# Four graph layers in one kernel: layer 2's second pass split in two, and the tangent sums centred by a matrix product

## The chip, the cores and the metric

The kernel runs on one core of a Trainium2 chip. The metric is device time in microseconds. Eight runs of the kernel before gave a median of 1151.43 us, from 1147.78 to 1156.36; one further execution was profiled.

## The reference

A matrix `x` of 4096 rows and 64 columns goes through four layers over one adjacency matrix `adj` of 4096 x 4096 zeros and ones (float32). Each layer's result is added to its input and every row is normalised.

```python
x = _layernorm(x + _L0_gnn_ref(x, adj, L0_gnn_W, L0_gnn_b), axis=-1)
x = _layernorm(x + _L1_gnn_ref(x, adj, L1_gnn_r, L1_gnn_w_att, L1_gnn_b_att), axis=-1)
x = _layernorm(x + _L2_gnn_ref(x, adj, L2_gnn_weight, L2_gnn_bias), axis=-1)
x = _layernorm(x + _L3_gnn_ref(x, adj, L3_gnn_att_w, L3_gnn_att_b), axis=-1)
```

Layer 0 averages the neighbours and multiplies by a weight. Layers 1 and 3 are hyperbolic attention: for every pair of rows a sigmoid of two scores, times the edge, weights a logarithm map of one row at the other; the weighted sum is a tangent, along which the row is then moved. Layer 2 weights a row's last neighbours by powers of one half, by their rank from the end of the row:

```python
support = input @ weight
mask = (adj != 0).astype(support.dtype)
rank = jnp.cumsum(mask, axis=1)
deg = rank[:, -1:]
k = jnp.minimum(deg, float(MAX_NEIGH))
pos = rank - (deg - k)
w = mask * jnp.where(pos > 0, DECAY ** (k - pos), 0.0)
out = w @ support + bias
```

## The kernel before, in words

The output rows are cut into four groups of 1024 (`GROUPS`, taken 3, 2, 1, 0) and the neighbours into 32 blocks of 128 (`BLOCKS`, taken 31 down to 0). `adj` lies transposed in memory, neighbours on partitions. `load` (L653) brings two blocks of one group, 1 MB, by SP's queue into one of six buffers; a layer needs 64 loads. Float32 edges are read as their upper bfloat16 halves. On 64 of the 256 loads, in layers 0 and 2, `check` (L739) has DVE test that all edges are 0 or 1 (L741).

**Layers 1 and 3.** `attend` (L914) works on one group: per block PE makes a score `z` [128, 1024] of three products for each half (L935, L938, L941), ACT a sigmoid (L943) and a square (L946), and DVE joins them (L949, and L951 for two blocks at once); PE then adds the weighted rows into `acc` [128, 512] (L955), the group's two halves above each other on the partitions. At the group's end ACT copies `acc` to `sums` (L962). `move` (L972) turns `sums` to rows by four PE transposes (L969), has ACT copy them out of PSUM (L985), forms `u` by taking each row's mean away (L988 reduce, L989 scale, L991 subtract, DVE), multiplies x by u (L992, POOL), squares u (L994, ACT), and after two reduces (L997, L999) runs a long chain of small operations on [128, 8] tiles, with `rsqrt` (L673 to L679) three times, to the new rows (L1067 POOL, L1068 and L1071 DVE). The sum of a row before centring is also used (L1001). Layer 1's rows then go through `linear` (L1074) into layer 2's `halves`; layer 3's go out by DMA (L1377).

**Layer 2.** Two groups are taken together, 3 and 2 in the first pass, 1 and 0 in the second. For each group and block PE counts in `z` [128, 1024], which is never cleared within a pass: the block before is passed by and this block enters, two products of 512 columns each (L1340). ACT makes the weights 2^-count by one exponential of 1024 (L1349), and PE adds `halves` times weights into the group's `acc` by four products, one group later (L1356, through `lag`). So each count waits for the exponential that read the same `z` before, and the two groups are two independent chains. `end_2` (L1288) turns the sums to rows (L969), adds bias and input, `norm_rows` (L761) normalises, and `prepare` (L781) makes the rows ready for layer 3: casts (L798 to L800), turned copies `hi_lo`, `lo_hi`, `src`, `dst` (L842 on PE, L846 on ACT), two logarithms (L849, L850), the scores, and for group 3 `left_b` (L904, L910).

**Order.** Row work is written as generators. `later` puts one into one of two queues, `tick` advances them a step each at fixed places of the block loops, `yield n` waits n ticks, and `need(tag)` runs them until a group's rows are ready. `take` and `free` share two PSUM buffers of one bank, `aux`, among them. In layers 0 and 2 PE and ACT follow the order as written (`tc.manual_schedule`); otherwise a planner orders each engine's instructions by its own estimates. Each engine then runs its list in order. The tiles of row work have one buffer each, so that a move's `u` is free only when the move before has used it up.

Of the kernel before, what the change touches and what calls it, by code (L numbers as in the profile page):

```python
# [10 lines left out]
F32 = mybir.dt.float32  # L11
# [47 lines left out]
def gnn_stack_kernel(  # L59
# [509 lines left out]
    def stream(fits):  # L569

        with ExitStack() as st:
# [127 lines left out]


# [271 lines left out]
            def move(layer, s, sums, curve):  # L972
# [7 lines left out]
                sum_1, k, d, uu = nums("sum_1"), nums("k"), nums("d"), nums("uu")  # L980
                u, w, sq, of = grp("u"), grp("w_att"), grp("sq"), grp("z0")
                yield from free()
                t = to_rows_of(sums)
                yield near()
                nc.scalar.copy(of.rearrange("p (h k) f -> p h k f", h=2), t)  # L985
                held.pop()
                yield near()
                V.tensor_reduce(sum_1, of, AX.X, ALU.add)  # L988
                V.tensor_scalar(k, sum_1, 1.0 / D, None, ALU.mult)  # L989
                yield soon()  # L990
                V.tensor_sub(u, of, over(k))  # L991
                nc.gpsimd.tensor_mul(w, xg, u)  # L992
                yield after(12)
# [315 lines left out]
            lag = []  # L1309

            def flush():

                while lag:
                    lag.pop(0)()

            with tc.manual_schedule(engines=FIXED):
                for n in range(0, NW, 2):
                    two = GROUPS[n : n + 2]
                    zs = [ps.tile([P, WW], F32, name="z") for _ in two]

                    accs = [[] for _ in two]
                    behind = [None, None]
                    for g in reversed(range(NB // 2)):
                        edges = []
                        for s in two:
                            a, edge = load(s, g)
                            if g % 2 == 1:
                                junk = sb.tile([P, 2, WW], F32, name="t").bitcast(BF16)
                                check(s, g, a, junk[:, 0, :].rearrange("p (b i) -> p b i", b=2))
                            edges.append(edge)  # L1330
                        need((2, 2 * g // WB))
                        for k in (1, 0):
                            j = 2 * g + k
                            for i, edge in enumerate(edges):
                                z, acc = zs[i], accs[i]
                                here = edge[:, k * WW : (k + 1) * WW]
                                for lhs, rhs in ((pass_by, behind[i]), (enter, here)):
                                    for h in range(0, WW, W):
                                        if rhs is not None:
                                            nc.tensor.matmul(  # L1340
                                                z[:, h : h + W], lhs, rhs[:, h : h + W],
                                                start=j == BLOCKS[0], stop=True,
                                                skip_group_check=True,
                                            )
                                behind[i] = here
                                flush()

                                w = sb.tile([P, 2, WW], F32, name="sq").bitcast(BF16)[:, 0, :WW]
                                nc.scalar.activation(w, z, AF.Exp, bias=at_edge, scale=-LN2)  # L1349

                                def add(acc=acc, j=j, w=w):
                                    if not acc:
                                        acc.append(ps.tile([P, W], F32, name="acc"))
# [112 lines left out]
```

## Time and profile before

| | us |
|---|---|
| median of eight runs | 1151.43 |
| lowest and highest of them | 1147.78, 1156.36 |
| the profiled execution | 1147.65 |
| its span | 1145.9 |
| layer 2, first pass and second pass (ends of the ACT copies L1370) | 104, 119 |
| layer 3, its four groups (ends of the ACT copies L962) | 105, 84.4, 80.9, 81.1 |
| after the last of them | 33.5 |

The span is what the profile covers; the execution's own time is 1.75 us longer. Engines are named as in the profile: PE is TensorE's matmul, PEld its weight load, DVE VectorE, ACT ScalarE, POOL GpSimd, SP the queue that issues the loads. A number in square brackets behind a row of the timeline is the idle time of the engine before that instruction, with the instruction that ended it.

### The profile page before, as it was taken

The numbers are of one execution on the slowest core, as the hardware profiler recorded it, in microseconds if no ns is written. First come the engines' busy times: TensorE is split into PE (matmuls) and PEld (weight loads), VectorE is DVE, ScalarE is ACT, GpSimd is POOL, SyncE is SP. The second block draws the span as 40 slices with busy tenths as digits, with TensorE's granted clock in tenths as the row PEclk, the third lists the DMA queues.
The fourth block names the chain that finished last, engine by engine and source line by source line (L and its number), as shares of the span: only waits on it lengthen the run. The fifth ranks groups of instructions, "written<-read, shape, count | busy, mean of one in ns | idle before, by whom it ended". The sixth has DMA issues, their size and how long they took to land.

```text
span 1145.9 us, 13431 instructions
## 1 busy us (share of the span) xinstructions
PE 1007.2 (88%) x4832; PEld 387.4 (34%) x4917; DVE 961.2 (84%) x1901; ACT 812.2 (71%) x823; POOL 61.1 (5%) x97
## 2 busy tenths in 40 slices
PE   6899897899899999988999988998798999999870
PEld 3445544233333333332333232333333333333220
DVE  6587898999999899989773584349988999999996
ACT  0003215899989788977767688887987999889860
POOL 0020120000000000000000020001000000000001
PEclk9999998999999999999999999999898999999995
DMA  9999998556566466644988886785355666666400
GB/s 351 421 379 411 364 414 321 202 169 217 198 208 219 162 209 208 216 172 149 322 298 301 324 305 242 258 339 184 110 183 174 222 209 209 219 209 207 150 0 22
DMA packets 38418, 271.57 MB, mean 237 GB/s; under 512 B 4550, under 2 KB 4550, under 8 KB 5574
## 3 DMA queue, kind: packets, MB, share of 16 engines
q1 hardware_dynamic: 37440, 269.50, 65.2%
q10 hardware_dynamic: 902, 1.12, 0.3%
q8 instruction: 40, 0.66, 0.2%
q14 instruction: 36, 0.29, 0.1%
HBM read 269.55 MB, written 1.05 MB: 236 GB/s over the span
## 4 chain that ended last, share of the span: by engine, by line
DVE 57%; PE 26%; ACT 6%; DMA 5%; issue 3%; POOL 2%; ACTq 0%; POOLq 0%; SPq 0%; DVEq 0%
DVE t L951 21%; DVE t L949 21%; PE z L1340 9%; PE acc L1356 5%; DMA edges<-in_adj_dram 4%; PE acc L955 3%; PE acc L1229 2%; DVE junk L741 2%; ACT sq L946 2%; ACT sq L1349 1%; PE z L938 1%; PE z L935 1%; PE z L941 1%; PE aux L1092 1%; DVE rs_t L677 1%
## 5 line engine op out<-in xcount | busy, mean ns | idle before, releaser
L943 ACT ACTIVATE sig<-left_b,right 128x1024 f32<-128x1024 f32 x256 | 293.9, 1149 | 45.1 <-DVE t L949 34.4
L949 DVE SCALAR_TENSOR_TENSOR t<-z,sig 128x1024 f32<-128x1024 f32 x256 | 310.2, 1217 | 14.9 <-ACT sq L946 14.1
L946 ACT ACTIVATE sq<-z,turn 128x1024 f32<-128x1024 f32 x256 | 281.6, 1106 | 28.0 <-PE z L941 25.8
L951 DVE SCALAR_TENSOR_TENSOR t<-sq,t 128x2048 f32<-128x2048 f32 x128 | 293.0, 2289 | 0.7
L955 PE MATMUL acc<-t,xe 128*64 128x512 f32 x1024 | 257.8, 616 | 34.1 <-DVE t L951 30.4
L935 PE MATMUL z<-edges,two_i 128*128 128x512 bf16 x464 | 183.9, 396 | 20.2 <-DVE t L949 20.0
L938 PE MATMUL z<-lo_hi,hi_lo 128*128 128x512 f16 x512 | 196.1, 383 | 3.7 <-issue 0.7
L941 PE MATMUL z<-dst,src 74*128 74x512 f16 x512 | 196.6, 384 | 0.0
L1349 ACT ACTIVATE sq<-z,at_edge 128x1024 bf16<-128x1024 f32 x128 | 141.9, 1114 | 55.2 <-PE z L1340 54.1
L955 PEld LDWEIGHTS acc<-t,xe 128*64 128x64 f32 x1024 | 63.5, 137 | 170.1 <-DVE t L951 89.3
L741 DVE SCALAR_TENSOR_TENSOR t<-edges 128x2048 bf16<-128x2048 f32 x32 | 73.8, 2313 | 46.8 <-DMA edges<-in_adj_dram 46.6
L935 PEld LDWEIGHTS <-two_i 128*128 128x128 bf16 x512 | 50.5, 99 | 141.0 <-issue 97.5
L1229 PE MATMUL acc<-edges,first 128*128 128x512 bf16 x241 | 76.8, 395 | 24.3 <-DMA edges<-in_adj_dram 23.8
L1356 PE MATMUL acc<-sq,halves 128*64 128x512 bf16 x512 | 80.1, 392 | 16.6 <-ACT sq L1349 15.3
L1229 PE MATMUL acc<-edges,third 128*65 128x512 bf16 x256 | 79.8, 393 | 0.6
L741 DVE SCALAR_TENSOR_TENSOR junk<-edges 128x2048 bf16<-128x2048 f32 x32 | 73.2, 2286 | 7.1 <-DMA edges<-in_adj_dram 6.9
L1340 PE MATMUL z<-edges,enter 128*128 128x512 bf16 x247 | 76.5, 388 | 0.3
L1340 PE MATMUL z<-edges,pass_by 128*128 128x512 bf16 x235 | 74.8, 394 | 1.8 <-issue 1.7
L938 PEld LDWEIGHTS <-hi_lo 128*128 128x128 f16 x512 | 50.6, 99 | 69.7 <-issue 26.5
L941 PEld LDWEIGHTS <-src 74*128 74x128 f16 x512 | 49.7, 97 | 69.7 <-issue 5.8
L1356 PEld LDWEIGHTS <-halves 128*64 128x64 f16 x512 | 19.2, 108 | 72.4 <-issue 72.3
L1229 PEld LDWEIGHTS <-first 128*128 128x128 bf16 x256 | 24.1, 98 | 52.7 <-issue 25.3
(260 smaller groups left out, 758.7 us busy)
## 6 DMA issues: line engine op xcount, KB each, us to landing
edges<-in_adj_dram SPq DMA_DIRECT2D x256, 1024.0 KB, 5.8
x<-in_x_dram SPq DMA_DIRECT2D x4, 256.0 KB
out_dram<-x ACTq DMA_DIRECT2D x4, 256.0 KB, 4.1
w_sb<-in_L_gnn_W_dram ACTq DMA_DIRECT2D x1, 32.0 KB, 4.7
given<-in_L_gnn_b_dram ACTq DMA_DIRECT2D x1, 0.2 KB
given<-in_L_gnn_bias_dram ACTq DMA_DIRECT2D x1, 0.2 KB
given<-in_L_gnn_b_att_dram ACTq DMA_DIRECT2D x1, 0.0 KB
given<-in_L_gnn_att_b_dram ACTq DMA_DIRECT2D x1, 0.0 KB
```

Of the source, the lines that this page charges most:

```text
L741: V.scalar_tensor_tensor(junk, a, 0.0, a, ALU.not_equal, ALU.not_equal, accum_out=odd[:, n : n + 1])
L935: nc.tensor.matmul(half, two_i, edge[:, at : at + W], start=True, stop=False)
L938: nc.tensor.matmul(half, hi_lo[:, of], lo_hi[:, to], start=False, stop=False)
L941: nc.tensor.matmul(half, src[:, of], dst[:, to], start=False, stop=True)
L943: nc.scalar.activation(sig, left_b, AF.Sigmoid, bias=right[:, j : j + 1])
L946: nc.scalar.activation(sq[:, k], zp, AF.Square, bias=turn, scale=-1.0 / UNIT)
L949: V.scalar_tensor_tensor(t[:, k], zp, 0.0, sig, ALU.max, ALU.mult)
L951: V.scalar_tensor_tensor(t, sq, HIGH**2, t, ALU.add, ALU.mult)
L955: nc.tensor.matmul(acc[h * D : (h + 1) * D, :], xe[:, j, :], t[:, k, h * W : (h + 1) * W], start=j == BLOCKS[0], stop=j == BLOCKS[-1],)
L1229: nc.tensor.matmul(accs[h][:m], lhs[:, j, :], edge[:, at : at + W], start=j == BLOCKS[0], stop=j == BLOCKS[-1],)
L1340: nc.tensor.matmul(z[:, h : h + W], lhs, rhs[:, h : h + W], start=j == BLOCKS[0], stop=True, skip_group_check=True,)
L1356: nc.tensor.matmul(acc[0][h * D : (h + 1) * D, :], halves[:, j, part * D : (part + 1) * D], w[:, h * W : (h + 1) * W], start=j == BLOCKS[0 ...
```

## The change

It has two parts. In layer 2 the first pass stays as it is (`wide_pass`). The second is split into two passes, for group 1 and then for group 0 (`narrow_pass`). In a narrow pass the group's two halves of 512 are the two chains: each has a `z` of its own with two count products per block and an exponential of 512, and the four add products of a block follow one block later. There is one tick per block, as there was one per group and block. `end_2` of group 1 is queued at the end of its own pass, thus ahead of group 0's.

In `move`, the four transposes, the reduce, the scale and the subtract are replaced by four products of `sums` with a constant matrix `centre` [128, 2, 65], that holds for each half the identity less 1/64 in 64 columns and ones in the last. So PSUM holds the centred row and its sum, 260 float32 for two of the four products; these go in two parts, each with an `aux` buffer and an ACT copy of its own, into one tile of [128, 8, 65], of which `u` and `sum_1` are views.

```diff
@@ -695,6 +695,16 @@
             V.tensor_scalar(two_i, ident, 2.0 * UNIT, None, ALU.mult)
             turn = num(keep, "turn", 1)
             V.memset(turn, ROOT + OFF)
+            centre = keep.tile([P, 2, D + 1], F32, name="centre")
+            V.memset(centre, 0.0)
+            for h in range(2):
+                of = slice(h * D, (h + 1) * D)
+                V.tensor_scalar(
+                    centre[of, h, :D], ident[of, of], -1.0 / D, None, ALU.add
+                )
+                V.memset(centre[of, h, D:], 1.0)
 
 
 
@@ -977,20 +987,24 @@
                 least = 1e-15 if layer == 1 else 1e-30
                 at = blocks(s)
                 xg, x2g = x_of(layer)[:, at, :], x2[:, at]
-                sum_1, k, d, uu = nums("sum_1"), nums("k"), nums("d"), nums("uu")
-                u, w, sq, of = grp("u"), grp("w_att"), grp("sq"), grp("z0")
-                yield from free()
-                t = to_rows_of(sums)
-                yield near()
-                nc.scalar.copy(of.rearrange("p (h k) f -> p h k f", h=2), t)
-                held.pop()
-                yield near()
-                V.tensor_reduce(sum_1, of, AX.X, ALU.add)
-                V.tensor_scalar(k, sum_1, 1.0 / D, None, ALU.mult)
-                yield soon()
-                V.tensor_sub(u, of, over(k))
+                k, d, uu = nums("k"), nums("d"), nums("uu")
+                w, sq = grp("w_att"), grp("sq")
+                all_u = row.tile([P, WB, D + 1], F32, name="u_1")
+                u, sum_1 = all_u[:, :, :D], all_u[:, :, D]
+                for part in range(2):
+                    yield from free()
+                    t = take(F32, P, 2, 2, D + 1)
+                    for i in range(2):
+                        cols = slice((2 * part + i) * P, (2 * part + i + 1) * P)
+                        nc.tensor.matmul(t[:, i], sums[:, cols], centre, start=True, stop=True)
+                    yield near()
+                    nc.scalar.copy(
+                        all_u.rearrange("p (h k) f -> p k h f", h=2)[:, 2 * part : 2 * part + 2], t
+                    )
+                    held.pop()
+                    yield near()
                 nc.gpsimd.tensor_mul(w, xg, u)
-                yield after(12)
                 nc.scalar.activation(sq, u, AF.Square)
                 yield near()
                 yield soon()
@@ -1306,68 +1320,98 @@
                 yield from norm_rows(3, s, z, x2[:, blocks(s)])
                 yield from prepare(3, s, att3, batt3_sb, curve3, 1e-30, good[:, 1], 40)
 
-            with tc.manual_schedule(engines=FIXED):
-                for n in range(0, NW, 2):
-                    two = GROUPS[n : n + 2]
...
+            def wide_pass(two):
+                zs = [ps.tile([P, WW], F32, name="z") for _ in two]
+                accs = [None, None]
+                behind, lag = [None, None], []
+                for g in reversed(range(NB // 2)):
+                    edges = [load_2(s, g) for s in two]
+                    need((2, 2 * g // WB))
+                    for k in (1, 0):
+                        j = 2 * g + k
+                        for i, edge in enumerate(edges):
+                            here = edge[:, k * WW : (k + 1) * WW]
+                            count(zs[i], behind[i], here, j, WW)
+                            behind[i] = here
+                            while lag:
+                                lag.pop(0)()
+                            w = weights_of(zs[i], WW)
+                            def add(i=i, j=j, w=w):
+                                if accs[i] is None:
+                                    accs[i] = ps.tile([P, W], F32, name="acc")
+                                add_up(accs[i], j, w[:, :W], w[:, W:])
+                            lag.append(add)
+                            if two[0] != GROUPS[0] or j < BLOCKS[4]:
+                                tick(1)
+                lag.pop(0)()
+                return accs
+            def narrow_pass(s):
+                zs = [ps.tile([P, WW], F32, name="z") for _ in range(2)]
+                acc = ps.tile([P, W], F32, name="acc")
+                behind, lag = [None, None], []
+                for g in reversed(range(NB // 2)):
+                    edge = load_2(s, g)
+                    for k in (1, 0):
+                        j = 2 * g + k
+                        w = sb.tile([P, 2, WW], F32, name="sq").bitcast(BF16)[:, 0, :WW]
+                        for h in range(2):
+                            here = edge[:, k * WW + h * W : k * WW + (h + 1) * W]
+                            count(zs[h], behind[h], here, j, W)
+                            behind[h] = here
+                            weights_of(zs[h], W, w[:, h * W : (h + 1) * W])
+                        if lag:
+                            add_up(acc, *lag.pop(0))
+                        lag.append((j, w[:, :W], w[:, W:]))
+                        tick(1)
+                add_up(acc, *lag.pop(0))
+                return [acc]
+            def load_2(s, g):
+                a, edge = load(s, g)
+                if g % 2 == 1:
+                    junk = sb.tile([P, 2, WW], F32, name="t").bitcast(BF16)
+                    check(s, g, a, junk[:, 0, :].rearrange("p (b i) -> p b i", b=2))
+                return edge
+            def count(z, behind, here, j, n):
+                for lhs, rhs in ((pass_by, behind), (enter, here)):
+                    for h in range(0, n, W):
+                        if rhs is not None:
+                            nc.tensor.matmul(
+                                z[:, h : h + W], lhs, rhs[:, h : h + W],
+                                start=j == BLOCKS[0], stop=True, skip_group_check=True,
+                            )
+            def weights_of(z, n, w=None):
+                if w is None:
+                    w = sb.tile([P, 2, WW], F32, name="sq").bitcast(BF16)[:, 0, :n]
+                nc.scalar.activation(w, z[:, :n], AF.Exp, bias=at_edge, scale=-LN2)
+                return w
+            def add_up(acc, j, *ws):
+                for part in range(2):
+                    for h, w in enumerate(ws):
+                        nc.tensor.matmul(
+                            acc[h * D : (h + 1) * D, :],
+                            halves[:, j, part * D : (part + 1) * D], w,
+                            start=j == BLOCKS[0] and part == 0,
+                            stop=j == BLOCKS[-1] and part == 1,
+                        )
             with tc.manual_schedule(engines=FIXED):
+                for some in (GROUPS[:2], GROUPS[2:3], GROUPS[3:]):
+                    accs = wide_pass(some) if len(some) == 2 else narrow_pass(some[0])
+                    for s, acc in zip(some, accs):
                         sums = row.tile([P, W], F32, name="sums", bufs=2)
+                        nc.scalar.copy(sums, acc)
                         later(end_2(s, sums))
```

`load_2`, `count`, `weights_of` and `add_up` hold the statements that stood in the loop before.

## The prediction

> **What bounds the kernel now.** I read the engine totals, then the busy time by stage, cut where an accumulator is copied out (ACT L962, L1370), then the timeline inside the stages that the change touches.
>
> ```profile
> PE 1007.2 (88%) x4832; PEld 387.4 (34%) x4917; DVE 961.2 (84%) x1901; ACT 812.2 (71%) x823; POOL 61.1 (5%) x97
> ```
>
> No engine bounds the whole. The stage rows give start:end, length, then busy us of PE, PEld, DVE, ACT and POOL:
>
> ```profile
> 537.00:641.00 104.00, 100.63 (x533) 33.59 (x544) 62.77 (x180) 72.26 (x74) 4.41 (x3) 1.00 0.85 297
> 641.00:761.00 120.00, 106.71 (x602) 35.59 (x613) 58.79 (x167) 95.78 (x98) 7.35 (x16) 0.99 0.80 285
> 761.00:866.00 105.00, 89.29 (x421) 34.24 (x427) 98.83 (x188) 91.72 (x93) 7.33 (x16) 0.93 0.54 186
> 950.40:1031.30 80.90, 75.74 (x327) 26.44 (x331) 80.77 (x117) 72.38 (x72) 2.32 (x2) 1.00 0.62 211
> 1112.40:1145.90 33.50, 0.93 (x5) 0.50 (x5) 22.37 (x128) 1.96 (x4) 4.38 (x3) 0.55 0.05 19
> ```
>
> Rows one and two are layer 2's passes: PE leads, DVE works only half the time. Rows three and four are layer 3's first and third attention group: DVE leads, and the first takes 24 us more than the third, because groups 1 and 0 are still being prepared there. The last row is the tail: one group's row arithmetic with PE done.
>
> The timeline shows layer 2's rhythm (start, length, engine, line):
>
> ```profile
> 690.41 0.62 PE L1356 MATMUL acc<-sq,halves 128*64 128x512 bf16 x4
> 690.97 0.63 PE L1340 MATMUL z<-edges,pass_by 128*128 128x512 bf16 x2
> 691.97 0.62 PE L1356 MATMUL acc<-sq,halves 128*64 128x512 bf16 x4
> 692.14 1.11 ACT L1349 ACTIVATE sq<-z,at_edge 128x1024 bf16<-128x1024 f32 x1 [0.45 <-PE z L1340]
> ...
> 700.46 1.28 ACT L943 ACT_TABLE_LOAD   x1
> ...
> 705.38 0.62 PE L1356 MATMUL acc<-sq,halves 128*64 128x512 bf16 x4 [3.03 <-ACT sq L1349]
> ```
>
> One block of one group takes 1.56 us (690.41 to 691.97): 1.00 for four count matmuls, 0.56 for four adds. ACT waits 0.45 per block, so PE sets the pace until ACT runs something else: at 700.46 a sigmoid of layer 3 comes between two exponentials with a table load on each side, and PE waits 3.03. The second pass is 64 x 1.56 = 100 plus 19: four such waits (2.56, 3.03, 2.27, 2.34) make 10.2, PE's own row work and restarts the rest.
>
> The tail by timeline:
>
> ```profile
> 1121.56 0.69 DVE L1071 TENSOR_TENSOR x<-u,w_att 128x512 f32<-128x512 f32 x1 [0.93 <-POOL w_att L1067]
> 1122.29 0.69 DVE L991 TENSOR_TENSOR u<-z,k 128x512 f32<-128x512 f32 x1
> 1123.12 1.26 POOL L992 TENSOR_TENSOR w_att<-x,u 128x512 f32<-128x512 f32 x1 [1.59 <-DVE u L991]
> 1124.42 0.69 DVE L999 TENSOR_REDUCE d<-w_att 128x8 f32<-128x512 f32 x1 [1.44 <-POOL w_att L992]
> ```
>
> Group 1's move ends at 1122.25, 11.9 after the last DVE L951 (1110.31), and group 0's u can only be formed then, though its sums had been turned by 1114.3.
>
> **What the Trainium skill says.** "ScalarE: Activation LUTs", What ACT_TABLE_LOAD costs, gives 1283 ns for a load plus a drain of about 1380. The load agrees (1283 at L943, L849 and L1349); the drain does not show: the load at 700.46 is followed by its sigmoid at 701.75. The same section prices an activation with a pointer bias at 280 ns + 0.833 per element, with an overlap of 93 ns: 1133 for 1024 elements, where the trace has 1114 (L1349). For 512, which the trace lacks, it gives 706; scaled to the trace I take 0.69 us, and 0.62 less overlap. "TensorE: Matmul & The Clock Gate", Part 1, says that PE falls to half clock after an idle window of about 3.4 us. The trace agrees loosely: after the 3.03 wait the next pairs of count matmuls take 0.93 and 1.05 instead of 0.61.
>
> **The change, part by part.** The orders come from the built instruction streams.
>
> 1. Layer 2's last two groups go one after the other. The 64 loads, 32 checks (L741) and PE's count and add matmuls are as many as before; SP takes group 1's 16 loads and then group 0's, at the same 3.12 us per load and through the same six buffers, so I cost the queue at nothing; PE's pace hides it, and if the DMA fell behind the price would be its lag. What changes is ACT and the distance between a half and its next use.
> (a) 128 exponentials of 512 take the place of 64 of 1024. ACT needs 0.69 + 0.62 = 1.31 per block, not 1.11; slack falls from 0.45 to 0.25. A half's loop is 0.5 of count, 0.15 to the last matmul's end, 0.1 to ACT, 0.69 and 0.06 back (as 705.32 to 705.38): 1.5 against the 1.56 that PE needs; the second half also queues behind the first's exponential, some 0.04 over. 64 x 0.04 = 2.5; bounds 0 and 10.
> (b) ACT's row work now lands on PE. Each 1.0 us copy of turned rows (L846) left no PE gap of 0.6 before; now it costs an estimated 0.3 beside PE's own 0.46 of transposes: 12 copies, 3.6. Three sets of casts (L798 to L800, 1.55 each) add 0.5 each: 1.5. The four table stalls lengthen by 0.3: 1.2.
> (c) Group 1's rows come into layer 2: PE 4 x 0.46 + 0.2 (L854) + 0.6 (L969) = 2.6, and a Ln with one table load at the very end, 1.0. One pass boundary more: 0.8.
> Sum +13; some of (b) is absorbed where transposes and copy meet, so I take **+11**, bounds +4 and +28.
>
> 2. Layer 3's first group then prepares group 0 alone. One group's DVE work there is eleven wide operations less overlap, 6.3, and about 55 small ones at 0.1: 12, half of the 24 excess; ACT loses a Ln/sigmoid pair of loads (2.6) inside it. DVE was on the path, so **-12**, bounds -7 and -16. Late next: group 0's rows, which are needed for the last four loads.
>
> 3. Each move (L972) loses a reduce (L988, 0.68), a scale (0.15) and a subtract (L991, 0.69) on DVE: 1.3 after overlap. Three moves run in layer 1's attention groups and three in layer 3's, where DVE is busy 80.77 of 80.90: 6 x 1.3 = 7.8. Against it, DVE's new order does the moves earlier: in layer 1 and layer 3 each, some 35 small operations of group 1's move come back into the attention groups (before: after the last block), 2 x 35 x 0.075 = 5.2 if none hides. PE is busy 75.74 of the same 80.90, so not all saved DVE time is time. Net -2.6; I take **-4**, since the two POOL waits behind L992 (1.4 each, DVE idle) can also be covered; bounds -14 and +4. ACT gains 2 x 0.38 (as L1102) for 0.58, +0.18 a move; PE turns by four 128x130 float32 products for four transposes of 0.66 together: the nearest row (L1186, 271 ns against 272) says no change, bounds 0 and +0.6 each, under ACT's copy. POOL reads u with a stride: 0, up to +0.3. The centre's constants are six small DVE operations at the start, +0.3, under the first load.
>
> 4. The tail. Group 1's move has only its last quarter left after the last block: three rsqrt steps to its final u took 4.2 (1134.31 to 1138.50) and the rest to 1140.85 2.35, so u is free 6.5 after the last L951 instead of 11.9. The ACT copies into u, waiting for that, take 0.76, as L991 did. **-5.4**, bounds -2 and -7.
>
> Sum: 11 - 12 - 4 - 5.4 = -10.4. The profiled execution is 1147.65 (span 1145.9), so 1137.3; the median of the runs, 1151.43, stands 3.8 above it, and I carry the difference over: 1141. A measurement of this kernel tells about 0.3%, 3.5 us.
>
> **Rivals.**
> A. Forecast: narrow passes cost some 11, returned by layer 3 and the tail: 1141, chance 0.50, own range 1134 to 1148.
> B. The narrow loops hold PE's pace and DVE's POOL waits at a move's start go too: passes +5, moves -10, tail and layer 3 as above: -22, **1129**. For it: ACT has 0.25 of slack and DVE is the bound in six groups. Against: PE is busy for 94% of such a group. Chance 0.23.
> C. ACT becomes the bound in the narrow passes. If a half's return costs 0.3 more than PE's 1.56 (a hand-over of 0.2 for my 0.1 and 0.06, and half clock after each stall), 64 x 0.3 = 19 come on top of 11: +30 - 21.4 = +8.6, **1160**. It decides from 0.17 us per block (10.4/64) as no gain at all. For it: 1.5 of 1.56 is close and 1.0 us copies stand in the same queue. Against: PE, not ACT, waited in no clean block. Chance 0.15.
> D. The passes do not do what they say for the end: DVE's order delays group 1's or 2's rows, PE waits for them in layer 2 as it did at 798.80 (2.9) in layer 3, and layer 3's gain is paid ahead: passes +18, **1148 to 1152**. Chance 0.12.
>
> **Numbers.** B and the lower three quarters of A are faster by over 0.3% with part of D: 0.72; same 0.12 (D, A's edge, C's lower part); slower 0.16. The range 1125 to 1156 leaves out C's upper half and B's far end.
>
> **What would show it.** Per block PE at 1.56 to 1.65 in the narrow passes, and the two together 125 to 137 long (120 before); the exponential of 512 at 0.69; the first group of layer 3 near 93; later groups near 80; DVE's L1013 within 9 us of the last L961 (14.1 before); one table load fewer. I am wrong if PE waits for ACT in most narrow blocks, if it waits for rows there, or if the groups of layers 1 and 3 do not shorten.

## The result, and the profile after

The kernel after took 1143.6 us in the median of 21 runs (1137.23 to 1146.7), beside 1151.75 for 58 runs of the kernel before: a ratio of 0.9926, 95% interval 0.9913 to 0.994. The gain of 8.2 us is real and small; 1141 was predicted. Its profiled span is 1140.3 us, for 1145.9 before. The profiles differ by 5.6 and the medians by 8.2, because the profiled execution of the kernel before lay some 4 us below its median and that of the kernel after 1.5 below.

The engine totals of the kernel after:

```profile
PE 1013.5 (89%) x4864; PEld 391.5 (34%) x4949; DVE 956.8 (84%) x1882; ACT 820.8 (72%) x894; POOL 66.2 (6%) x97
```

Again no engine bounds the whole. DVE lost 4.4 us of busy time and ACT gained 8.6. The busy time by stage, kernel after, with the columns of the prediction's stage rows (start:end, length, PE, PEld, DVE, ACT, POOL, then granted clock, DMA share, GB/s):

```profile
539.90:644.70 104.80, 102.72 (x544) 34.46 (x554) 54.39 (x138) 72.96 (x77) 4.31 (x3) 1.00 0.84 302
644.70:705.60 60.90, 54.08 (x304) 18.52 (x310) 45.21 (x141) 49.47 (x80) 8.86 (x16) 1.00 0.84 295
705.60:776.60 71.00, 59.95 (x336) 20.00 (x341) 30.09 (x92) 62.34 (x94) 2.73 (x8) 0.93 0.70 242
776.60:867.70 91.10, 81.72 (x376) 29.74 (x383) 88.05 (x126) 83.55 (x83) 3.18 (x8) 1.00 0.58 199
949.00:1030.10 81.10, 76.63 (x332) 26.95 (x336) 79.96 (x114) 72.68 (x72) 4.88 (x2) 1.00 0.62 211
1115.00:1140.30 25.30, 1.53 (x9) 1.05 (x9) 15.18 (x83) 1.49 (x4) 4.15 (x3) 0.55 0.07 25
```

Layer 2's second pass of 119.1 has become two of 60.9 and 70.9, 12.7 longer together. Layer 3's first group, 105 before, takes 91.1. So the two effects of the split nearly cancel. The third group is as long as before. Cut at the last DVE operation of the last block (L961 here, L951 before), which no later step can move, the table is:

| us, one profile each | before | after | difference |
|---|---|---|---|
| layer 0 | 181.7 | 183.6 | +1.9 |
| layer 1, four groups | 356.0 | 356.3 | +0.3 |
| layer 2, first pass | 104.9 | 104.8 | -0.1 |
| layer 2, groups 1 and 0 | 119.1 | 131.8 | +12.7 |
| layer 3, group 3 | 105.0 | 91.2 | -13.8 |
| layer 3, groups 2, 1 and 0, to the last L961 | 243.7 | 243.0 | -0.7 |
| from there to the end | 35.6 | 29.6 | -6.0 |

Layer 0 has nothing new but the five small DVE operations that build `centre` (0.66 us together). It took 179.5 to 185.1 in the kernels profiled here, both ends in kernels that have `centre`, so its +1.9 can't be put down to the edit.

The rhythm of a narrow pass, from the kernel after's timeline:

```profile
656.84 0.62 PE L1401 MATMUL acc<-sq,halves 128*64 128x512 bf16 x4
...
658.11 1.27 ACT L1395 ACTIVATE sq<-z,at_edge 128x512 bf16<-128x512 f32 x2 [0.29 <-PE z L1386]
...
658.41 0.62 PE L1401 MATMUL acc<-sq,halves 128*64 128x512 bf16 x4
...
659.69 1.27 ACT L1395 ACTIVATE sq<-z,at_edge 128x512 bf16<-128x512 f32 x2 [0.31 <-PE z L1386]
```

A clean block is still 1.57 us (656.84 to 658.41), and ACT, with two exponentials in 1.27, still waits 0.3 for PE. The lost time is elsewhere, where ACT has other work. First, at group 3's casts:

```profile
663.99 1.54 DVE L805 TENSOR_TENSOR y<-x,ym 128x512 f32<-128x512 f32 x1
...
665.56 0.62 ACT L808 CAST ys<-y 128x512 f16<-128x512 f32 x1 [1.47 <-DVE y L805]
...
667.85 0.39 PE L1386 MATMUL z<-edges,pass_by 128*128 128x512 bf16 x1 [2.55 <-ACT sq L1395]
```

ACT reached the casts before DVE had made their input. It stood for 1.47 and then cast for 1.56, with the next exponentials queued behind, so PE stood for 2.55. Second, at layer 3's sigmoids, which the planner puts into this pass:

```profile
706.82 1.28 ACT L953 ACT_TABLE_LOAD   x1
708.12 1.15 ACT L953 ACTIVATE sig<-left_b,right 128x1024 f32<-128x1024 f32 x1
709.28 1.28 ACT L1395 ACT_TABLE_LOAD   x1
...
711.32 0.58 PE L1386 MATMUL z<-edges,pass_by 128*128 128x512 bf16 x1 [2.71 <-ACT sq L1395]
...
719.07 0.58 PE L1386 MATMUL z<-edges,pass_by 128*128 128x512 bf16 x1 [3.04 <-ACT sq L1395]
```

A sigmoid and two loads keep ACT from layer 2 for 3.7 us, twice. After each wait PE's matmuls start at 0.58 apiece, where 0.39 is the usual.

The tail of the kernel after; its last L961 ends at 1110.70:

```profile
1116.44 0.69 DVE L1085 TENSOR_TENSOR x<-u,w_att 128x512 f32<-128x512 f32 x1 [0.94 <-POOL w_att L1081]
1117.23 0.38 ACT L1002 COPY u<-aux 128x260 f32<-128x260 f32 x1 [2.24 <-DVE x L1085]
...
1117.50 0.38 ACT L1002 COPY u<-aux 128x260 f32<-128x260 f32 x1
...
1117.96 1.18 POOL L1007 TENSOR_TENSOR w_att<-x,u 128x512 f32<-128x512 f32 x1 [1.55 <-ACT u L1002]
...
1119.17 0.69 DVE L1013 TENSOR_REDUCE d<-w_att 128x8 f32<-128x512 f32 x1 [0.54 <-POOL w_att L1007]
```

Group 1's move gives up `u` 6.4 after the last block (1117.13; 11.9 before), the centred rows are copied in at once, and L1013 starts 8.5 after the last block, for 14.1 before.

### The profile page after: what moved, and what is told of

Read it like the earlier page. It is cut to its first block, busy times and chain, and to the rows that moved or that the text cites. A ratio compares the mean times of both kernels' runs of the same rounds, so it can differ in the third digit from the quotient of the medians.

```text
span 1140.3 us, 13541 instructions
## 1 busy us (share of the span) xinstructions
PE 1013.5 (89%) x4864; PEld 391.5 (34%) x4949; DVE 956.8 (84%) x1882; ACT 820.8 (72%) x894; POOL 66.2 (6%) x97
## 3 DMA queue, kind: packets, MB, share of 16 engines
HBM read 269.55 MB, written 1.05 MB: 237 GB/s over the span
## 4 chain that ended last, share of the span: by engine, by line
DVE 55%; PE 27%; ACT 9%; DMA 4%; POOL 2%; issue 2%; ACTq 0%; SPq 0%; POOLq 0%; DVEq 0%
DVE t L959 21%; DVE t L961 20%; PE z L1386 9%; PE acc L1401 5%; DMA edges<-in_adj_dram 4%; PE acc L1243 3%; PE acc L965 3%; ACT sig L953 2%; DVE junk L751 2%; ACT sq L956 2%; ACT sq L1395 2%; PE aux L1106 1%; PE z L945 1%; POOL sq L778 1%; PE aux L852 1%
## 5 line engine op out<-in xcount | busy, mean ns | idle before, releaser
L961 DVE SCALAR_TENSOR_TENSOR t<-sq,t 128x2048 f32<-128x2048 f32 x128 | 293.0, 2289 | 0.7
L965 PE MATMUL acc<-t,xe 128*64 128x512 f32 x1024 | 255.4, 612 | 29.6 <-DVE t L961 24.4
L948 PE MATMUL z<-lo_hi,hi_lo 128*128 128x512 f16 x512 | 193.8, 379 | 3.3 <-issue 0.3
L951 PE MATMUL z<-dst,src 74*128 74x512 f16 x512 | 195.0, 381 | 0.0
L1395 ACT ACTIVATE sq<-z,at_edge 128x512 bf16<-128x512 f32 (+1 forms) x192 | 152.8, 830 | 50.7 <-PE z L1386 48.3
L1386 PE MATMUL z<-edges,pass_by 128*128 128x512 bf16 x242 | 87.2, 398 | 16.9 <-ACT sq L1395 15.8
L1386 PE MATMUL z<-edges,enter 128*128 128x512 bf16 x239 | 83.9, 392 | 0.3
L951 PEld LDWEIGHTS <-src 74*128 74x128 f16 x512 | 49.1, 96 | 67.4 <-issue 2.1
L1081 POOL TENSOR_TENSOR w_att<-x,p 128x512 f32<-128x512 f32 x8 | 12.9, 1616 | 497.3 <-DVE q L1079 497.3
```

Source lines behind the costliest of these rows:

```text
L948: nc.tensor.matmul(half, hi_lo[:, of], lo_hi[:, to], start=False, stop=False)
L951: nc.tensor.matmul(half, src[:, of], dst[:, to], start=False, stop=True)
L961: V.scalar_tensor_tensor(t, sq, HIGH**2, t, ALU.add, ALU.mult)
L965: nc.tensor.matmul(acc[h * D : (h + 1) * D, :], xe[:, j, :], t[:, k, h * W : (h + 1) * W], start=j == BLOCKS[0], stop=j == BLOCKS[-1],)
L1386: nc.tensor.matmul(z[:, h : h + W], lhs, rhs[:, h : h + W], start=j == BLOCKS[0], stop=True, skip_group_check=True,)
L1395: nc.scalar.activation(w, z[:, :n], AF.Exp, bias=at_edge, scale=-LN2)
```

## The experiments

Ratios are to the kernel before on the same chip, with 95% intervals.

**Each part alone.** e1_centre_only is the kernel before with the new `move`; layer 2 keeps its second pass of two groups. e2_narrow_only has the two narrow passes and the old `move`. Against the kernel after:

```diff
 # e1_centre_only: layer 2 as before
-                for some in (GROUPS[:2], GROUPS[2:3], GROUPS[3:]):
-                    accs = wide_pass(some) if len(some) == 2 else narrow_pass(some[0])
+                for n in range(0, NW, 2):
+                    two = GROUPS[n : n + 2]
...
 # e2_narrow_only: move as before
-                        nc.tensor.matmul(t[:, i], sums[:, cols], centre, start=True, stop=True)
...
+                t = to_rows_of(sums)
...
+                V.tensor_reduce(sum_1, of, AX.X, ALU.add)
+                V.tensor_scalar(k, sum_1, 1.0 / D, None, ALU.mult)
...
+                V.tensor_sub(u, of, over(k))
```

> Centring product in the moves, layer 2 as before (two wide passes). Theory T (the split of the pass pays back in layer 3's first group what it costs in layer 2, and the net gain is the shorter move in the tail): layer 2's second pass 119, layer 3's first group 104, tail after the last block 30 instead of 35.6; total 0.5% below before, some 1145. Rival R1 (the gain comes from preparing group 1 in layer 2, the centring only moves work around): within 0.2% of before, 1150 or more. Rival R2 (both parts give about half): 1147 to 1148.

> Narrow passes for groups 1 and 0, moves as before (transposes, reduce, scale, subtract). Theory T: passes together 131, layer 3's first group 91, everything else as before: 1150 to 1151, a difference of 0.1% from before that cannot be told. R1: 0.7% below before, 1144. R2: 1147 to 1148.

e1 took 1142.89, 0.9923 (0.9901 to 0.9945); e2 took 1151.97, 1.0004 (0.9988 to 1.0021). In this kernel the whole gain belongs to the centring, and the split is worth nothing. Their stage rows, first e1 (second pass, then layer 3's first group):

```profile
644.90:767.60 122.70, 110.15 (x599) 35.94 (x609) 58.78 (x167) 95.19 (x97) 7.34 (x16) 0.94 0.76 277
767.60:872.10 104.50, 86.83 (x419) 32.38 (x425) 99.27 (x189) 91.62 (x95) 7.33 (x16) 0.97 0.51 187
```

and e2 (group 0's narrow pass after 62.0 for group 1's, then layer 3's first group):

```profile
708.10:779.00 70.90, 60.01 (x336) 20.08 (x341) 30.04 (x92) 62.16 (x93) 2.39 (x8) 0.93 0.66 240
779.00:870.20 91.20, 81.81 (x377) 29.76 (x383) 88.16 (x126) 83.66 (x84) 3.17 (x8) 1.00 0.55 200
```

The two stages together are 227.2 in e1 and 224.1 in e2, for 224.1 before and 223.0 after. What leaves layer 3's first group turns up in layer 2: in layer 3's first group DVE has 99.27 us of work in e1 and 88.16 in e2. From layer 3's second group to the end e1 takes 272.5, as the kernel after does (272.6), and e2 280.2 (279.3 before). This difference lies after the last block: up to there the four kernels take 242.9, 243.0, 242.6 and 243.7.

**Are DVE's two saved operations the gain?** e4_two_more_dve gives each move of the kernel after a reduce and a subtract whose results nothing reads.

```diff
                 nc.scalar.activation(sq, u, AF.Square)
+                spare, unused = nums("spare"), grp("unused")
+                V.tensor_reduce(spare, u, AX.X, ALU.add)
+                V.tensor_sub(unused, u, over(spare))
```

> The changed kernel, with a reduce and a subtract of 128x512 put back on DVE in each of the eight moves; nothing reads their results. Theory D (DVE sets the attention groups' pace, the saved operations are time): 1.3 for each of six moves and for the one in the tail, 8 to 10 above the changed kernel, 1152. Rival P (the groups are paced by the ring of PE, ACT and DVE with slack at DVE; the saved operations were covered): 0 to 3 above, 1144 to 1147.

It took 1145.78, 0.9948 (0.9932 to 0.9964): 2.2 us above the kernel after, with intervals that overlap. That lies within rival P's 0 to 3, far from theory D's 8 to 10. The profile tells more. Layer 3's groups 2, 1 and 0, up to the last block:

```profile
869.69:1114.96 245.27, 225.02 (x963) 78.76 (x977) 242.35 (x364) 211.50 (x205) 7.15 (x5) 0.99 0.50 179
```

The eight kernels profiled here that have the new move, with one buffer for `u`, take 242.8 to 243.0 for this. So three moves' two operations, 4.1 us of DVE's time, cost 2.3, and the fourth move adds 0.6 after the last block. Layer 1, with three moves too, took 354.2, not more but 2.1 less. So the operations have a price in layer 3, about half of their duration, and none that shows in layer 1. With both put back, layer 3 from its second group to the end takes 275.5, still 3.8 below the 279.3 before. So they are less than half of the centring's gain there. Whether the rest comes from the scale, the shorter way from PSUM to `u`, the `yield after(12)` that fell away or the order that the planner then finds, no run tells apart.

**Is the tail's gain the early `u`?** e8_before_two_u gives the kernel before a second buffer for `u` and `w_att`, so that group 0's `u` needn't wait for group 1's move.

```diff
-                u, w, sq, of = grp("u"), grp("w_att"), grp("sq"), grp("z0")
+                u, w, sq, of = grp("u", 2), grp("w_att", 2), grp("sq"), grp("z0")
...
-                    at, rest = blocks(s), grp("u")
+                    at, rest = blocks(s), grp("u", 2)
```

> The kernel before with two buffers each for u and w_att in the moves, nothing else. Theory U (the tail is bound by the single u: the last group's move can only begin when the move before has used it up): the tail after the last block falls from 35.6 to 28 to 30, total 5 to 8 below before, 1144. Rival O (it is DVE's planned order that puts the last group's operations behind; the buffer only follows it): tail within 2 of 35.6, total within 3 of before.

It took 1150.56, 1.0004 (0.9981 to 1.0027). The stretch after the last block did fall from 35.6 to 29.7, the kernel after's own value. But layer 3's third group rose from 80.9:

```profile
952.30:1038.20 85.90, 79.08 (x333) 27.08 (x331) 83.34 (x125) 72.81 (x72) 4.91 (x2) 0.96 0.56 199
```

DVE does in the group what it no longer does at the end: 83.34 us here, for 80.77 before. Starting `u` early only moves DVE's work to a place where DVE is also late. So it was neither theory as it stood: the tail fell as theory U says, the total stayed as rival O says. An early `u` pays if there is also less of that work, and the centring gives that in part (e4).

**What makes the narrow passes longer?** e3_no_early_sigmoid holds layer 3's first two sigmoids behind the last copy of layer 2. e5_wide_no_early_sigmoid does the same in e1, with the two-group pass.

```diff
-                        nc.scalar.activation(
-                            sig, left_b, AF.Sigmoid, bias=right[:, j : j + 1]
-                        )
+                        with ExitStack() as behind:
+                            if layer == 3 and s == GROUPS[0] and g == NB // 2 - 1:
+                                behind.enter_context(tc.issue_after(last_2[-1].ins))
+                            nc.scalar.activation(
+                                sig, left_b, AF.Sigmoid, bias=right[:, j : j + 1]
+                            )
...
-                        nc.scalar.copy(sums, acc)
+                        last_2.append(nc.scalar.copy(sums, acc))
```

> The changed kernel, with layer 3's first two sigmoids held behind layer 2's last copy, so that they no longer stand between the exponentials of group 0's pass. Theory S (each of these two interruptions costs PE two table loads, the sigmoid and then some microseconds at a lower clock): group 0's pass shrinks from 70.9 to about 61, layer 3's first group grows by 1 to 2 for the sigmoids, total 7 to 9 below the changed kernel, 1135. Rival (the pass is held by row work that would wait elsewhere; the interruptions are cover for it): 0 to 3 below, 1141 to 1144.

> Centring product with layer 2's second pass wide as before, and the two early sigmoids held behind layer 2's last copy. Theory T (the narrow passes pay back in layer 3 exactly what they cost): second pass 113 (119 to 123 less the two interruptions), layer 3's first group 106; total within 3 of the changed kernel without early sigmoids (1134.9): 1135 to 1138. Rival N (the narrow passes lost mainly by those interruptions, which a chain of half the slack answers with a longer stall, and are worth something without them): 1140 or more here.

e3 took 1134.89, 0.9864 (0.9842 to 0.9885). Group 0's pass and layer 3's first group:

```profile
705.40:768.20 62.80, 57.44 (x336) 19.54 (x341) 29.93 (x92) 54.64 (x86) 6.67 (x8) 0.97 0.76 269
768.20:862.10 93.90, 83.54 (x375) 30.05 (x383) 89.25 (x126) 85.49 (x85) 3.67 (x8) 0.96 0.54 195
```

The pass falls by 8.1 and the group after it gives 2.8 back. But e5 took 1134.38, 0.9876 (0.9844 to 0.9908), no worse, and its second pass is 114.5 long:

```profile
640.30:754.80 114.50, 107.60 (x611) 35.39 (x610) 58.68 (x167) 87.80 (x92) 7.34 (x16) 0.99 0.82 295
```

The early sigmoids cost either form some 8 us (8.7 and 8.5 between the medians), and the two forms stay level without them.

**The other table switch.** e6_one_table is e3 with one table set for exp and ln loaded ahead of the narrow passes; e9_wide_one_table does so in e5.

```diff
+                    if some == GROUPS[2:3]:
+                        nc.scalar.preload_act_table_set("natural_log_exp_and_others")
                     accs = wide_pass(some) if len(some) == 2 else narrow_pass(some[0])
```

> The changed kernel without early sigmoids, and with one table that holds exponential and logarithm loaded ahead of the narrow passes, so that the two logarithms of each group need no switch. Theory S (a switch is a stall of PE in a narrow pass: 2.5 for the pair of loads, and a lower clock at times): 2.5 in group 1's pass, 4 in group 0's, total 5 to 7 below 1134.9, 1129. Rival (PE's stall at the logarithm is the wait for row work, not the loads): 0 to 2 below.

> Centring product, second pass wide, no early sigmoids, and one table for exponential and logarithm from the second pass on. Theory T (the narrow passes pay back in layer 3 what they cost in layer 2, in any company): two switches fewer, 2.3 each: second pass 110, layer 3's first group 105, total 1130, within 3 of the same thing with narrow passes (1130.2). Rival N (the narrow passes were held up by switches more than the wide ones, so without switches they are ahead): 1134 or more here.

e6 took 1130.2, 0.983 (0.9799 to 0.9861), and its timeline shows the logarithms between two exponentials with no load on either side:

```profile
731.11 0.21 ACT L859 ACTIVATE tt<-tt 128x8 f32<-128x8 f32 x1
731.21 0.21 ACT L860 ACTIVATE q<-q 128x8 f32<-128x8 f32 x1
731.42 1.26 ACT L1399 ACTIVATE sq<-z,at_edge 128x512 bf16<-128x512 f32 x2
```

The program's table loads fall from 14 in e3 to 10, and group 0's pass from 62.8 to 58.2; the median falls by 4.7, a little less than the 5 to 7 expected. The Trainium skill ("ScalarE: Activation LUTs", Table sets) says that `natural_log_exp_and_others` holds both functions, so that the pair needs one load; this run agrees. e9 took 1135.83, 0.9868 (0.9843 to 0.9893), no better than e5. This isn't theory T's 1130 but lies where rival N was put (1134 or more), and the second passes with layer 3's first group are 213.1 in e6 and 217.6 in e9. That suggests that the split has some 4 us to give once no switch is left inside it. But the two intervals overlap, and the two profiled spans are equal (1131.6 and 1131.4), mostly since layers 0 and 1 took 3.3 longer in e6's. So this isn't settled.

**The form against the rows.** e10_rows_late is e3 with group 1's row work queued only after group 0's pass, and its casts and logarithms held behind layer 2's last copy. So the narrow passes do the row work that the two-group pass does.

```diff
...
+                        if s == GROUPS[2]:
+                            sums_1 = sums
+                            continue
+                        if s == GROUPS[3]:
+                            later(end_2(GROUPS[2], sums_1))
                         later(end_2(s, sums))
```

> The changed kernel without early sigmoids, with narrow passes as they are, but group 1's row work queued after group 0's pass, so that layer 3's first group does it, as before the change. Theory M (of the 12 that the narrow passes cost, about half is group 1's row work that moved in, half is their form: longer stalls and one more boundary): the two passes fall from 125.2 to 119 to 120, where the wide pass without early sigmoids took 114.4; layer 3's first group rises from 93.9 to about 106; total 1140 to 1142. Rival F (the form costs all of it): passes stay at 124 or more, total 1146. Rival W (the moved row work costs all of it): passes 115, total 1136.

It took 1141.56, 0.9923 (0.9897 to 0.9948). Its passes take 120.7 together, for 114.5 in e5 (two-group pass) and 125.2 in e3 (with the rows). So without the sigmoids, by one profile each, the form costs some 6.2 and the moved rows 4.5. Between the medians e10 lies 7.2 above e5, which has the same rows in the same places, though the intervals overlap a little. Layer 3's first group, with the rows back in it:

```profile
766.20:869.80 103.60, 90.81 (x425) 34.39 (x424) 91.85 (x134) 93.49 (x96) 2.62 (x8) 0.92 0.50 179
```

It is 9.7 longer than e3's. In e5, where the two-group pass leaves it the same row work, this group takes 104.8.

**Two chains or one.** e7_one_chain gives a narrow pass one `z` of 1024 and one exponential of 1024 per block.

```diff
...
-                        for h in range(2):
-                            here = edge[:, k * WW + h * W : k * WW + (h + 1) * W]
-                            count(zs[h], behind[h], here, j, W)
-                            behind[h] = here
-                            weights_of(zs[h], W, w[:, h * W : (h + 1) * W])
+                        here = edge[:, k * WW : (k + 1) * WW]
+                        count(z, behind, here, j, WW)
+                        behind = here
+                        weights_of(z, WW, w)
```

> The changed kernel, with the narrow passes counting both halves in one z and one exponential of 1024, as one chain. Theory C (a chain's loop is count, 0.25 of hand-over out, exponential, 0.06 back; two chains hide each other's exponential, one chain cannot): a block takes 1.0 + 0.25 + 1.11 + 0.06 = 2.4 instead of 1.57, the two passes grow by 64 x 0.85 = 54 less what the row work then hides, some 45; total 1180 to 1195. Rival (PE's own work sets the pace in any form): passes within 5 of 131.8.

One execution took 1173.22, less than the 1180 to 1195 expected. The block is 2.32 us (657.58 to 659.90), the exponential's 1.11 and PE's 1.21 one behind the other:

```profile
657.58 1.11 ACT L1394 ACTIVATE sq<-z,at_edge 128x1024 bf16<-128x1024 f32 x1 [1.21 <-PE z L1385]
...
658.74 0.61 PE L1385 MATMUL z<-edges,pass_by 128*128 128x512 bf16 x2 [0.71 <-ACT sq L1394]
...
659.90 1.11 ACT L1394 ACTIVATE sq<-z,at_edge 128x1024 bf16<-128x1024 f32 x1 [1.21 <-PE z L1385]
```

The two passes take 161.8. So the halves as chains keep the split from costing 30 us more; 45 had been expected.

**The fastest version.** e11_one_table_two_u is e6 with a second buffer for `u_1` and `w_att`.

```diff
-                w, sq = grp("w_att"), grp("sq")
+                w, sq = grp("w_att", 2), grp("sq")
...
-                all_u = row.tile([P, WB, D + 1], F32, name="u_1")
+                all_u = row.tile([P, WB, D + 1], F32, name="u_1", bufs=2)
```

> The fastest kernel so far (narrow passes, no early sigmoids, one table) with two buffers for u and w_att in the moves. Theory D (time in the last groups and the tail is DVE's work plus the waits on its chain; the single u only shifts where it shows): the tail falls by 1 to 3 and the groups before it rise by as much, total within 2 of 1130.2. Rival U (the single u costs the tail 1.2 of waiting for L1085, with nothing given back): 1 to 2 below 1130.2 with the groups of layer 3 unchanged.

It took 1129.22, 0.9801 (0.9777 to 0.9825), within 1 us of e6. Both beat the kernel before and the kernel after; between the medians the second buffers add nothing that can be told. In the profile it isn't as theory D says: layer 3's groups up to the last block fell, to 240.7, and the tail is 29.7, much as in the kernel after.

## Why the prediction was right, and where its terms were off

The forecast, rival A, held: 1143.6 against 1141, by the mechanism that it named: layer 3's first group returns what the narrow passes cost, and the tail gets shorter. Two of its four terms were right (steps 2 and 4), one was right in sum and wrong in its parts (step 1), which is luck in part, and one was too large (step 3).

**Step 1, the split (+11).** The profiles of the kernels before and after say +12.7. Over more profiles, the mean of three with the two-group pass (before, e8, e1: 119.1, 120.7, 122.7) is 120.8 and of three with narrow passes (after, e2, e4: 131.8, 132.9, 134.4) is 133.0: +12.2. PE's clock has a share in it. The mean granted clock of these passes is 0.99, 0.99 and 0.94 in the first three and 0.96, 0.95 and 0.94 in the others; times the length, that is some 3.4 and 6.8 us of clock lost on average. So up to 3.4 of the 12.2 is clock, an estimate; outside rival C the prediction has no term for it. The parts were other than said:
- (a) The chain of a half: 2.5 was taken; 64 clean blocks at 1.57 for 1.56 make 0.6. ACT's slack is 0.3, as said (0.25).
- (b) The copies of turned rows: 3.6 was taken; 0.3 shows. Blocks that hold a copy (L856) take 1.56 to 1.58, but for one of 1.85; those with PE's own transposes take 2.0 to 2.1 (one 2.59, at half clock), and those existed before.
- (b) The casts: 1.5 was taken for three sets, half a microsecond each. Group 3's alone cost 1.95, because ACT also waited 1.47 for DVE's L805. The prediction didn't think of an ACT instruction of the row work that waits at the head of the queue and holds up two exponentials.
- (b) The table stalls: 1.2 was taken, as 0.3 more waiting at each of four. At the logarithms PE waits no longer than before (2.56 and 2.34 before, 2.46 twice after), but the two blocks around each take 6.24 for 5.73, which is 1.0 for both. The stretch with the two sigmoids costs 11.0 beyond its five blocks, for 7.35 before (both with group 2's casts in it), and there too the waits grew little: 3.03 and 2.27 before, 2.71 and 3.04 after. This is the term that was most too small, and what it left out is the clock (shown below).
- (c) The moved rows: 3.6 was taken with their logarithms; e10 measures 4.5. The boundary: 0.86 for 0.8.

The stretch with the two sigmoids, before, then after; the granted clock is the third number from the end:

```profile
700.72:715.87 15.15, 9.62 (x48) 3.21 (x49) 5.12 (x5) 13.99 (x14) 0.00 (x0) 0.89 0.66 236
707.39:726.26 18.87, 12.76 (x52) 3.88 (x52) 13.52 (x34) 15.13 (x20) 1.04 (x1) 0.73 0.35 123
```

PE had half clock for 3.4 us of the first and for 10.2 of the second, and was busy in 3.2 and 9.0 of them. At half pace that is some 2.9 us more, an estimate, of the 3.65; longer waits are 0.45 and PE's own row work 0.5.

0.6 + 0.3 + 1.95 + 1.0 + 3.65 + 4.5 + 0.86 is 12.9, so the sum of the readings is near the measured +12.7, with half a microsecond of row work in it twice. Without sigmoids and rows these readings leave 4.7 for the form, where e10 and e5 differ by 6.2. PE's clock may be the other 1.5: in e10's passes PE had half clock for 6.8 us, in e5's for 3.4 (mean 0.97 and 0.99). The sum was met by luck: copies that cost almost nothing made up for sigmoids and casts that cost more. Rival C, ACT as the bound, fell: its extra 0.3 per block is 0.01. Rival D fell too: in these passes no PE wait for late rows appears, and the one late row operation, L805, held ACT. Of rival B one half was right, the narrow hold; what it left out is what ACT has to do between the exponentials.

**Step 2, layer 3's first group (-12).** Measured -13.8 in the two profiles; e10 against e3, where nothing but group 1's rows differs by design, says 9.7. Both lie within the bounds given. It nearly repays step 1, and e2 shows the balance in the medians: 1.0004.

**Step 3, the moves (-4).** This is the mis-sized term: +0.3 in layer 1 and -0.7 in layer 3 make -0.4. A saved operation was priced too high: 1.3 was taken for the three of a move, 1.2 of it for the two that e4 puts back, and e4 grew by about 0.8 a move in layer 3's groups and not at all in layer 1's. And the work that moves up was put too low. In layer 1's groups and layer 2's first pass, the kernel before:

```profile
181.70:537.60 355.90, 325.23 (x1440) 118.21 (x1464) 337.20 (x483) 308.10 (x301) 10.15 (x14) 0.99 0.58 201
537.60:642.50 104.90, 101.88 (x541) 34.03 (x551) 62.17 (x177) 72.96 (x76) 4.41 (x3) 1.00 0.85 300
```

and layer 1's groups in the kernel after:

```profile
183.60:539.90 356.30, 325.49 (x1453) 119.97 (x1478) 338.95 (x508) 307.82 (x306) 12.01 (x14) 0.99 0.58 198
```

Three moves saved 3 x 1.52 = 4.6 of DVE's busy time there (0.68 + 0.15 + 0.69 each). Yet DVE is busy for 338.95 instead of 337.20, so 6.3 moved in, not 2.6. They came from layer 2's first pass, where DVE fell from 62.17 to 54.39, and where it had been idle almost half the time: that pass didn't shorten. So half of the step's expected -4, layer 1's, became nothing that shows. (Layer 1 took 356.0 to 359.5 in three profiles with the old move and 354.2 to 357.7 in ten with the new, so a gain of a microsecond there isn't excluded.) The half for layer 3 came in at -0.7. Of the small terms, the products of `centre` take PE 1.05 to 1.42 a move for the transposes' 0.60 to 0.66, so they came in near the upper bound of +0.6. POOL's product of x and u takes 1.59 on average for 1.28, its bound of +0.3; but POOL's other product (L1067, now L1081), with operands as before, grew as much, so the stride isn't shown to be the reason.

**Step 4, the tail (-5.4).** -6.0 by the last block. `u` is free 6.4 after it (6.5 said) and L1013 comes at 8.5 (within 9 said). e8 adds what the step left out: the tail alone can be had by a second buffer, and is then paid in the groups before. In layer 3, steps 3 and 4 are one account. The groups up to the last block and the tail, before, then after:

```profile
866.59:1110.31 243.72, 225.82 (x950) 77.72 (x965) 238.01 (x334) 210.92 (x202) 5.92 (x5) 0.98 0.53 180
1110.31:1145.93 35.62, 2.86 (x13) 0.98 (x13) 24.22 (x142) 2.22 (x5) 4.38 (x3) 0.58 0.05 18
867.73:1110.70 242.97, 223.79 (x963) 78.08 (x977) 239.04 (x358) 211.41 (x206) 9.27 (x5) 1.00 0.53 181
1110.70:1140.34 29.64, 5.13 (x17) 1.81 (x17) 18.82 (x107) 2.08 (x5) 4.30 (x3) 0.56 0.06 22
```

DVE's busy time in the groups went from 238.01 to 239.04, although three moves there save 4.6: so 5.6 moved in. Most of it came from the tail, where DVE's work fell from 24.22 to 18.82, 1.5 of that saved and 3.9 moved. As in layer 1 the saved time was filled with later work; but here that was work of the tail, where PE has almost nothing left to do, and the tail got shorter. Together the two are 279.3 before and 272.6 after, -6.7, where -7.4 had been said (half of -4, and -5.4).

The sum of the four terms by the profiles is 12.7 - 13.8 - 0.4 - 6.0 = -7.5, for -10.4 predicted and -8.2 between the medians.

The single checks: clean blocks at 1.57 (1.56 to 1.65 said), the passes together 131.8 (125 to 137), the exponential of 512 at 0.69 (0.69), layer 3's first group 91.2 (near 93), its later ones near 81 (near 80), and one table load fewer (19 to 18).

What stays open is whether the split would pay in a kernel without table switches (e6 and e9), what of the centring beside the two operations shortens the tail (e4), and why the planner places the sigmoids early; no run touched its estimates.

## What to carry to other kernels

Work saved on an engine paid here only where that engine ends last, and then about half of its duration. It is worth nothing if the saving lets work move up from a stage in which the engine was idle: look at the busy time of the stage after, too. Work moved from one stage to another has to be priced twice, where it leaves and where it arrives, and splitting a loop to move it can come out at zero. Before reshaping a loop that lives on a steady return from one engine, look for foreign instructions in that engine's queue: here two early sigmoids with their table loads, which no part of the change touched, were worth as much (8.7 us, e3 beside the kernel after) as the whole change.

## What the runs showed of the hardware that was not expected

PE ran at half pace after waits shorter than the window of about 3.4 us that the Trainium skill gives ("TensorE: Matmul & The Clock Gate", Part 1): 0.58 to 0.63 for a matmul of 512 instead of 0.39, after waits of 2.71 and 3.04. These waits ended at 711.32 and 719.07 in the kernel after, and the granted clock agrees:

```profile
711.40:714.80 3.40, 3.04 (x9) 0.77 (x10) 2.79 (x4) 3.38 (x7) 1.04 (x1) 0.50 0.29 63
714.80:718.20 3.40, 1.23 (x7) 0.33 (x6) 3.06 (x13) 3.37 (x3) 0.00 (x0) 1.00 0.59 246
718.20:725.00 6.80, 5.93 (x20) 1.51 (x20) 5.05 (x14) 4.14 (x7) 0.00 (x0) 0.50 0.46 157
```

It isn't a matter of length alone. In layer 2's second passes, half clock followed a wait of 2.55 in e2 and e4 but not in the kernel after, and waits of 2.34 twice in e1 but not at all in e8; the shortest wait that it followed is 2.05, in e6. Likewise PE waited for 2.82 in the kernel before and 2.81 in the kernel after at the last block of all, and the eight adds that follow took 1.94 in the one and 3.59 in the other. Those 1.7 us cost nothing here, as the rows then waited for `u` until 1117.13. What decides whether half clock follows, no run shows. One stage of the same code can thus differ between profiles: group 1's narrow pass took 60.9 at a mean clock of 1.00 in the kernel after, and 62.0 at 0.97 in e2. So a stage's granted clock has to be read beside its length.
